# Spreading per-row values along the columns with VectorE's block transposes in place of matmuls with ones

## The chip, the cores and the metric

The kernel runs on one core of one Trainium2 chip. The time is device microseconds of one execution, start to end. Before the change three runs gave 2766.16, 2765.39 and 2765.9 us, median 2765.9. A profiled execution is looked at in detail; its own time was 2766.02 us, and the span from its first to its last instruction 2764.3 us.

## The reference, cut to what matters

128 graphs of 64 nodes with 512 features go through four layers; each layer is `x = layernorm(x + layer(x))`. Everything is float32. Three places take a value per node and need it once per row and once per column of the graph's 64x64 matrix:

```
# layer 0, a hypergraph convolution (twice): H = (adj != 0), D_i = sum_e H[i,e] * adj[0,e], B_e = sum_i H[i,e]
m   = 1/B[:, None] * (H^T @ (x @ W^T));   out = 1/D[:, None] * (H @ m) + b
# layer 1, scores of all pairs
y = x @ w;  s = y @ a
A = s[:, None] + s[None, :];  A = tanh(A / 8) * 8;  A = where(A >= 0, A, 0.1 * A)
A = exp(A) * adj
A = A / A.sum(-1, keepdims) * adj.sum(-1, keepdims)
out = A @ x @ w
# layer 2: three graph convolutions with relu; layer 3: attention with eight heads, adj and exp(-adj) added
```

The kernel keeps the graph matrices transposed (row: the node that is summed over; column: the node that receives), because a matmul sums over rows. So 1/D, the second s and the divisor of the row sums are all needed along the columns, while VectorE makes them as one value per partition.

## The kernel before

Two graphs lie on the 128 partitions (a pair), and four pairs make a group of 512 rows; 16 groups are worked in turn. A value per node is a tile `[128, 4]`, a graph matrix of a group `[128, 4, 64]`.

The products with the 512-wide weights are made in `multiply` (L551) in seven block products instead of eight: each block product is four matmuls of 128x128 by 256 columns, accumulated in PSUM tiles a, c and b (`a_l2c`, `c_l2c`, `b_l2c` for the product l2c, in the order B11, T1, T2, B21, T3, B22, T4). Between them VectorE or ScalarE takes snapshots (u) and sums out of PSUM, and a following block product on the same tile waits for that. PSUM has four such accumulators (pool `ps_acc`) and four more tiles (pool `ps_gt`) for transposes, graph products and the matrices of this change.

Three groups are in flight: side a (`first_half`) takes a group through layers 0 and 1, side b (`second_half`) takes the group before it through layer 2 and to the scores of layer 3, and t, the end of the same generator, finishes the group before that. A written list of steps (`order`, L1394) interleaves them; a step like a.ss is the stretch up to that `yield`. `start` does the same for the first group, where `strict` keeps TensorE, VectorE and ScalarE in the order of the text; in these parts the profile shows L132 for every instruction. After that a scheduler may move instructions on an engine against the text, by its own estimate of when operands are ready. `behind(key)` holds an instruction back: it is issued after the one recorded in `last_add` under that key.

How a value gets along the columns, in all three places: VectorE multiplies the identity (`identc`, L103, the unit matrix of each half stacked) with the value broadcast over 64 columns, which gives a diagonal matrix (`dg` L657 for 1/D, `e` L811 for the scores); TensorE multiplies it with `bones` (L93), a block matrix of ones, so every row gets the diagonal (`rbps` L663, `ss` L818); then it is taken out of PSUM (`rb` by ScalarE L668, or directly in the addition for `t`, L823). For the row sums of layer 1 the matmul with `bones` does the summing too: `den` (L831) sums t over its rows and gives each row the result, VectorE takes the reciprocal of all 128x256 (L836) and multiplies (L837). Group 0 does the scores and the division in two halves of two pairs (`attention`, `divided`).

```
t = tanh(ss + s4)          L823, L824
t = max(0.1 t, t)          L825
t = exp(8 t)               L826
t = t * atc                L827, atc: adj transposed
```

The steps around it in the steady list are

```
load a.w21 b.gh a.w2 rows b.l2c1 b.l2c2 a.ss b.l2c t.o1 a.den t.o2 a.c3 b.agg t.o a.p1 b.xT ... b.k1 prep b.k b.dots
```

`rows` makes the next group's H, its sums and 1/D (`prepare`, L618) and `prep` its `sps` and `smat`, the matrix of layer 0. a.c3 multiplies x by t (`gt_l`, L486); b.agg is layer 2's last sum over neighbours (L1148) and its addition to x (L1153); t.o is layer 3's output product (`a_wo`, `b_wo`, `c_wo`). The b side's addition out of c_l2c (L578) is `behind("e_...")`: VectorE does it after e of the other side. Weights come by SP's DMA queue into a ring of 20 tiles, asked for as tiles come free.

Of the kernel before, what the change touches and what calls it, by code (L numbers as in the profile page):

```python
# [41 lines left out]
def kernel(  # L42
# [48 lines left out]
    make_identity(nc, ident)  # L91

    bones = const.tile([P, 2, C], FP, name="bones")  # L93
    nc.vector.memset(bones, 0.0)
    nc.vector.memset(bones[0:C, 0, :], 1.0)
    nc.vector.memset(bones[C:P, 1, :], 1.0)
    ones = const.tile([P, P], FP, name="ones")
# [452 lines left out]

    def multiply(lefts, wt_q, dst, key, flipped=False, res=None, stops=(3,), then=None):  # L551

# [38 lines left out]
        last_add[f"{key}.p6"] = newest(PE)  # L591
        last_add[key] = vec.tensor_add(dst(0, 1), pc, s2).ins  # L592
        if then:
# [19 lines left out]
    def turned(t):  # L613

        return lambda m, n: t[:, 2 * n : 2 * n + 2, m * Q : (m + 1) * Q]


    def prepare(g):  # L618
# [24 lines left out]
        if q == 0:  # L643
            inverse(inv[:, 1], db[:, 1])
        else:
            by_rows()

            with behind(f"e_{q - 1}") if q > 2 else nullcontext():
                vec.tensor_mul(hn[:, 1], hn[:, 0], g["wb"])
                vec.reduce_sum(db[:, 0], hn[:, 1], axis=AX.X)  # L650
                inverse(inv, db)
        cs = small.tile([P, G], FP, name=f"cs_{q}", tag="cs")
        g["cs"], g["rowsum"] = cs, rowsum
        if q > 0:
# [6 lines left out]
        if q > 0:  # L661
            rb_ps = ps_gt.tile([P, G, C], FP, name=f"rbps_{q}", tag="gt")
# [70 lines left out]
    def first_half(g):  # L733
# [71 lines left out]
        for p in range(G):  # L805
# [4 lines left out]
        e = grp.tile([P, G, C], FP, name=f"e_{q}", tag="e", bufs=1)  # L810
        last_add[f"e_{q}"] = vec.tensor_mul(  # L811
            e, identc.unsqueeze(1).to_broadcast([P, G, C]), bcast(s4, G)
        ).ins
        yield "w2"

        ss = ps_gt.tile([P, G, C], FP, name=f"ss_{q}", tag="gt")
        with behind("l2c_0.p5") if q == 1 else nullcontext():
            ten.matmul(  # L818
                ss.rearrange("p a i -> p (a i)"), bones.rearrange("p g j -> p (g j)"),
                e.rearrange("p a i -> p (a i)"), start=True, stop=True,  # L820
            )
        t = grp.tile([P, G, C], FP, name=f"t_{q}", tag="t", bufs=1)
# [8 lines left out]
        ten.matmul(  # L831
            den.rearrange("p a i -> p (a i)"), bones.rearrange("p g j -> p (g j)"),
            t.rearrange("p a i -> p (a i)"), start=True, stop=True,
        )
        rd = grp.tile([P, G, C], FP, name=f"rd_{q}", tag="rd", bufs=1)
        vec.reciprocal(rd, den)  # L836
# [21 lines left out]
        with behind(f"q_{q - 1}.d"):  # L858
            rest()
        yield "ln1"  # L860


# [27 lines left out]
    def first_group(g):  # L890
# [71 lines left out]
        t = grp.tile([P, G, C], FP, name="t_0", tag="t", bufs=1)  # L962
        rd = grp.tile([P, G, C], FP, name="rd_0", tag="rd", bufs=1)
        mvs = [small.tile([P, 2, 2], FP, name=f"mv_l0_0_{d}", tag="mvp") for d in range(2)]
# [8 lines left out]
        def scored(d):  # L973
            rs = root(mvs[d], f"l0_0_{d}")
            vec.reciprocal(rs, rs)
            for p in range(2 * d, 2 * d + 2):
                normed(pair(p), mvs[d], rs, p % 2)
            for p in range(2 * d, 2 * d + 2):
                prod = work.tile([P, D], FP, name=f"xwa_0_{p}", tag="w")
                vec.scalar_tensor_tensor(  # L980
                    prod, pair(p), 1.0, wa_bc, ALU.mult, ALU.mult, accum_out=s4[:, p : p + 1]
                )
            at = slice(2 * d, 2 * d + 2)
            vec.tensor_mul(e[:, at], identc.unsqueeze(1).to_broadcast([P, 2, C]), bcast(s4[:, at], 2))

        def attention(d):
            at = slice(2 * d, 2 * d + 2)
            ss = ps_gt.tile([P, 2, C], FP, name=f"ss_0_{d}", tag="gt")
            ten.matmul(
                ss.rearrange("p a i -> p (a i)"), bones.rearrange("p g j -> p (g j)"),  # L990
                e[:, at].rearrange("p a i -> p (a i)"), start=True, stop=True,
            )
            vec.tensor_add(t[:, at], ss, bcast(s4[:, at], 2))
            act.activation(t[:, at], t[:, at], AF.Tanh, scale=0.125)
            vec.scalar_tensor_tensor(t[:, at], t[:, at], 0.1, t[:, at], ALU.mult, ALU.max)
            act.activation(t[:, at], t[:, at], AF.Exp, scale=8.0)
            vec.tensor_mul(t[:, at], t[:, at], g["atc"][:, at])

        def divided(d):
            at = slice(2 * d, 2 * d + 2)  # L1000
            den = ps_gt.tile([P, 2, C], FP, name=f"den_0_{d}", tag="gt")
            ten.matmul(
                den.rearrange("p a i -> p (a i)"), bones.rearrange("p g j -> p (g j)"),
                t[:, at].rearrange("p a i -> p (a i)"), start=True, stop=True,
            )
            vec.reciprocal(rd[:, at], den)
            vec.tensor_mul(t[:, at], t[:, at], rd[:, at])

# [12 lines left out]
        yield "w23"  # L1021
        divided(0)
        yield "den0"
        out_of_2(3, rows_of(3, hts, w2, 1, 2, ps))
# [8 lines left out]
        def out_of_l1(p):  # L1033
            ps = rows_of(p, [left.t], by_pairs[w_l1])
            vec.scalar_tensor_tensor(
                pair(p), ps.rearrange("p n f -> p (n f)"), g["rowsum"][:, p : p + 1], pair(p), ALU.mult, ALU.add
            )
            st = small.tile([P, 6], FP, name=f"st_l1_0_{p}", tag="st")
            stats(mvs[p // 2], st, p % 2, pair(p))
# [12 lines left out]
        yield "l11"  # L1052
        divided(1)
        yield "den1"
        normed_l1(0)
# [9 lines left out]
    def second_half(g):  # L1065
# [74 lines left out]
        for duo in range(2):  # L1140
# [3 lines left out]
            for h in range(2):  # L1144
                for p in range(2):
                    rows = slice(p * C, (p + 1) * C)
                    mat = g["atc"][rows, 2 * duo + p, :] if p == h else g["atx"][rows, duo, :]
                    ten.matmul(  # L1148
                        ps[p][h * C : (h + 1) * C, :], mat, g3[rows, 2 * duo + h, :], start=True, stop=True
                    )  # L1150
            for p in range(2):
                xr = xg[:, 2 * duo + p, :]
                vec.tensor_add(xr, ps[p], xr)  # L1153
        yield "agg"
# [226 lines left out]
    def taken(duo, ps, left):  # L1381
# [8 lines left out]
        a0.c1 prep0 keep0 rest a0.w1a keep1 a0.w1b rows0 bw0 a0.c20 wa bw0 a0.c21 doubled0 constant0 rows1 a0.w20 keep2 wa  # L1390
        a0.w21 prep1 a0.w22 a0.ss0 a1.c1 a0.w23 a0.den0 doubled1 a0.w24 a0.c30 a1.w1a1 a0.l10 a0.ss1 a0.l11 a0.den1 a1.w1a2
# [62 lines left out]
    for n, (who, q, name) in enumerate(todo):  # L1454
# [7 lines left out]
        elif who == "rows":  # L1462
            if q > 0:
                preps[q] = prepare(groups[q])
            with behind(f"l0w2_{q - 1}" if q > 2 else "q_0") if q > 1 else nullcontext():
                next(preps[q])
        elif who == "prep":
            next(preps[q])
# [93 lines left out]
```

## Time and profile before

| | |
|---|---|
| median of three runs | 2765.9 us |
| the profiled execution, and its span | 2766.02, 2764.3 us |
| TensorE busy, share of the span | 2743.0 us, 99% |
| VectorE | 2024.8 us, 73% |
| ScalarE | 808.2 us, 29% |
| one step of the steady list (the product l0w of one group to that of the next, 996.83 to 1167.37 and 1167.37 to 1337.13 in the chain) | about 170 us |
| granted TensorE clock | 1.0 |

An f32 matmul leaves two records on TensorE. A record's duration includes what the pipeline overlaps with the next, so the time that a matmul costs is read from start to start. "PE" is TensorE, "DVE" VectorE, "ACT" ScalarE, "PEld" the loading of weights into TensorE. A name like `t<-ss,s` is output and inputs; buffer and group numbers are left out.

### The profile page before, as it was taken

How to read it: one execution, taken by the hardware profiler on the slowest of the kernel's cores; microseconds unless marked ns; L12 is line 12 of the kernel's file. 1: busy time of each engine (PE TensorE's matmuls, PEld its weight loads, DVE VectorE, ACT ScalarE, POOL GpSimd, SP SyncE). 2: the span in 40 equal slices, each digit the busy share in tenths (PEclk: the TensorE clock that was granted, in tenths of full speed). 3: DMA queues.
4: the chain of work that ended last, by engine and by line, in shares of the span. 5: the costliest groups of instructions: out<-in, count | busy, mean ns of one | idle time of the engine just before them, and what ended most of it. 6: DMA issues, size and time to landing. Idle time of an engine off the chain costs nothing.

```text
span 2764.3 us, 67699 instructions
## 1 busy us (share of the span) xinstructions
PE 2743.0 (99%) x28868; PEld 2364.3 (86%) x28868; DVE 2024.8 (73%) x3883; ACT 808.2 (29%) x1459; POOL 38.0 (1%) x71
## 2 busy tenths in 40 slices
PE   9999999999999999999999999999999999999998
PEld 7888888888888888888888888888888888888887
DVE  6868687776777777777776767778777687776766
ACT  3223223232232322322233232232322323132232
POOL 2000000000000000000000000000000000000000
PEclk9999999999999999999999999999999999999999
DMA  8535454454544545445454454545545454454541
GB/s 270 171 119 157 128 170 135 138 165 133 166 127 141 165 127 168 128 145 165 132 164 130 142 161 132 162 126 152 158 135 164 131 156 145 127 165 130 150 124 61
DMA packets 309388, 405.15 MB, mean 147 GB/s; under 512 B 57408, under 2 KB 185184, under 8 KB 309088
## 3 DMA queue, kind: packets, MB, share of 16 engines
q1 hardware_dynamic: 304256, 385.58, 47.4%
q0 software_dynamic: 4832, 15.24, 1.5%
q8 instruction: 229, 3.75, 0.6%
q14 instruction: 71, 0.58, 0.1%
HBM read 369.78 MB, written 30.93 MB: 145 GB/s over the span
## 4 chain that ended last, share of the span: by engine, by line
PE 98%; DVE 1%; ACT 0%; issue 0%; DMA 0%; DVEq 0%
PE a_l0w L544 15%; PE b_l0w L544 7%; PE a_l2b L544 4%; PE a_q L544 4%; PE a_k L544 4%; PE a_l2c L544 4%; PE a_l2a L544 4%; PE a_v L544 4%; PE c_l0w L544 4%; PE a_l1w L544 4%; PE a_wo L544 4%; PE gt_l L486 3%; PE pp L132 3%; PE gt_l0h L486 2%; PE b_l2b L544 2%; PE b_q L544 2%
## 5 line engine op out<-in xcount | busy, mean ns | idle before, releaser
L544 PE MATMUL a_l0w<-w2w,aT_l0h 128*128 128x256 f32 x720 | 164.3, 381 | 0.0
L462 DVE BATCH_NORM_STATS2 st_l<-x 128x6 f32<-128x512 f32 x244 | 157.4, 671 | 0.1
L544 PEld LDWEIGHTS a_l0w<-w2w,aT_l0h 128*128 128x128 f32 x720 | 135.6, 190 | 18.8
L468 DVE TENSOR_SCALAR x<-x,mv_l,rs_l 128x512 f32<-128x512 f32 x244 | 119.1, 541 | 1.8
L544 PE MATMUL b_l0w<-w2w,s_l0h 128*128 128x256 f32 x480 | 108.5, 379 | 0.0
L763 ACT ACTIVATE h<-h 128x1024 f32<-128x1024 f32 (+1 forms) x58 | 54.9, 947 | 178.5 <-DVE h L592 157.5
L497 ACT COPY aT_l<-gt_l 128x512 f32<-128x512 f32 x148 | 78.4, 596 | 81.5 <-PE gt_l L486 81.5
L544 PEld LDWEIGHTS b_l0w<-w2w,s_l0h 128*128 128x128 f32 x480 | 91.1, 190 | 12.5
L1122 ACT ACTIVATE aT_h<-gth,gb_col 128x256 f32<-128x256 f32 x128 | 48.5, 492 | 159.0 <-PE gth L1114 159.0
L452 ACT ACTIVATE rs_l<-mv_l,eps_t 128x4 f32<-128x4 f32 (+1 forms) x64 | 19.1, 298 | 253.6 <-DVE mv_l L463 241.8
L559 DVE TENSOR_TENSOR u_l0w<-a_l0w,b_bc 128x512 f32<-128x512 f32 x56 | 38.5, 688 | 69.3 <-PE a_l0w L544 69.3
L544 PE MATMUL a_l2b<-gwbw,aT_h 128*128 128x256 f32 x360 | 86.6, 383 | 0.7 <-ACT aT_oT L1384 0.7
L544 PE MATMUL a_l2c<-gwcw,aT_h 128*128 128x256 f32 x360 | 86.6, 383 | 0.4 <-DVE g L584 0.4
L544 PE MATMUL a_q<-aT_xT,wqw 128*128 128x256 f32 x360 | 85.1, 379 | 0.7 <-ACT aT_xT L1172 0.7
L544 PE MATMUL a_l1w<-ww,aT_l 128*128 128x256 f32 x360 | 85.1, 379 | 0.2 <-ACT aT_l L497 0.2
L544 PE MATMUL a_l2a<-aT_l,gwaw 128*128 128x256 f32 x360 | 85.0, 379 | 0.0
L544 PE MATMUL a_k<-aT_xT,wkw 128*128 128x256 f32 x360 | 85.0, 379 | 0.0
L544 PE MATMUL a_l0w<-w1aw,aT_l 128*128 128x256 f32 x336 | 80.8, 383 | 0.0
L544 PE MATMUL a_v<-wvw,aT_xT 128*128 128x256 f32 x336 | 80.8, 383 | 0.0
L544 PE MATMUL a_wo<-wow,aT_oT 128*128 128x256 f32 x336 | 79.5, 379 | 0.1
L544 PE MATMUL a_l0w<-w1bw,aT_l 128*128 128x256 f32 x336 | 79.4, 379 | 0.0
L544 PEld LDWEIGHTS a_l2c<-gwcw,aT_h 128*128 128x128 f32 x360 | 66.4, 190 | 13.3 <-DVE g L584 3.7
(537 smaller groups left out, 6487.8 us busy)
## 6 DMA issues: line engine op xcount, KB each, us to landing
w2w<-w2k SPq DMA_DIRECT2D x210, 256.0 KB, 2.7
x<-in_x_dram SPq DMA_DIRECT2D x15, 1024.0 KB, 6.7
w1aw<-w1ak SPq DMA_DIRECT2D x60, 256.0 KB, 2.7
w1bw<-w1bk SPq DMA_DIRECT2D x60, 256.0 KB, 2.7
ww<-wk SPq DMA_DIRECT2D x60, 256.0 KB, 2.8
gwaw<-gwak SPq DMA_DIRECT2D x60, 256.0 KB, 3.9
gwbw<-gwbk SPq DMA_DIRECT2D x60, 256.0 KB, 2.6
gwcw<-gwck SPq DMA_DIRECT2D x60, 256.0 KB, 2.7
```

The costliest lines, as they stand in the source:

```text
L132: return op(*args, **kwargs)
L452: act.activation(rs[:, at], mv[:, at, 1], AF.Sqrt, bias=eps_t)
L462: vec.bn_stats(st, xg[:, p, :])
L468: vec.tensor_scalar(xg[:, p, :], xg[:, p, :], mv[:, p, 0:1], rs[:, p : p + 1], ALU.subtract, ALU.mult)
L486: ten.matmul(ps[g][f * C : (f + 1) * C, c, p, :], src(2 * duo + p)[rows, c0 : c0 + C], mat[rows, 2 * duo + p, :], start=True, stop=True,)
L497: act.copy(o[:, :, :, g, :], ps[g])
L544: ten.matmul(acc[:, blk, :], lhsT, rhs, start=(first and blk == 0 and i == 0), stop=(last and i == n_k - 1), skip_group_check=True,)
L559: last_add[f"{key}.{what}"] = (act.copy(t, ps) if res is None else vec.tensor_add(t, ps, res(m, n))).ins
L763: act.activation(hn, hn, AF.Relu)
L1122: act.activation(o[:, :, h, :], ps[h][:, c].rearrange("p (d a) i -> p d (a i)", d=2), AF.Relu, bias=gb2_col[:, k : k + 1],)
```

## The change

A new function `along(dst, src)` lays a value per node along the columns with VectorE alone. VectorE's transpose turns blocks of 32x32. `along` transposes the value, broadcast over 64 columns, for all 128 partitions at once: each block of 32 rows then has its own 32 values in both halves of its columns. Half of these blocks are right. Four more transposes, each of 32 partitions, overwrite the others with the values of the other 32 rows of the same graph.

It takes the place of the three matmuls: of `dg` and `rbps` and the copy for 1/D, of `e` and `ss` for the scores, and, for the divisor, VectorE multiplies exp's result also by `adn` (adj as it is; the scores are symmetric), sums along the columns (four values per partition), takes the reciprocal of those and lays them out. `bones` is gone. Group 0 doesn't lay the divisor out at all: `row_ratio` makes row sum over divisor per node, and the row scale that is applied after the product takes it.

The order changes with it. The 1/D part of `rows` becomes a step of its own, `rows2`, behind b.agg (for groups from 3 on); the points that hold work back move: the key `e_q` now marks the addition of t, and the addition that takes b_l2c out is held behind t's division. a.den comes before b.l2c, and group 1's a.c3 goes behind group 0's agg matmuls.

```diff
+    def along(dst, src):
+        n, B = src.shape[1], 32
+        vec.transpose(dst, bcast(src, n))
+        for g in range(2):
+            for b in range(2):
+                here, there = (slice(g * C + k * B, g * C + (k + 1) * B) for k in (b, 1 - b))
+                done = vec.transpose(
+                    dst[there, :, b * B : (b + 1) * B], src[here].unsqueeze(2).to_broadcast([B, n, B])
+                )
+        return done
...
# multiply
-        last_add[key] = vec.tensor_add(dst(0, 1), pc, s2).ins
+        with behind(held):
+            last_add[key] = vec.tensor_add(dst(0, 1), pc, s2).ins
...
# prepare
-            with behind(f"e_{q - 1}") if q > 2 else nullcontext():
+            if q > 2:
+                yield
+            with behind(f"agg_{q - 2}") if q > 2 else nullcontext():
...
-            dg = grp.tile([P, G, C], FP, name=f"dg_{q}", tag="dg", bufs=1)
-            vec.tensor_mul(dg, identc.unsqueeze(1).to_broadcast([P, G, C]), bcast(inv[:, 0], G))
+            rb = grp.tile([P, G, C], FP, name=f"rb_{q}", tag="rb", bufs=1)
+            along(rb, inv[:, 0])
...
-            ten.matmul(
-                rb_ps.rearrange("p a t -> p (a t)"), bones.rearrange("p g j -> p (g j)"),
-                dg.rearrange("p a t -> p (a t)"), start=True, stop=True,
-            )
-            rb = grp.tile([P, G, C], FP, name=f"rb_{q}", tag="rb", bufs=1)
-            act.copy(rb, rb_ps)
...
# first_half
-        last_add[f"e_{q}"] = vec.tensor_mul(
-            e, identc.unsqueeze(1).to_broadcast([P, G, C]), bcast(s4, G)
-        ).ins
+        along(e, s4)
+        t = grp.tile([P, G, C], FP, name=f"t_{q}", tag="t", bufs=1)
+        last_add[f"e_{q}"] = vec.tensor_add(t, e, bcast(s4, G)).ins
...
-            ten.matmul(
-                ss.rearrange("p a i -> p (a i)"), bones.rearrange("p g j -> p (g j)"),
-                e.rearrange("p a i -> p (a i)"), start=True, stop=True,
-            )
-        vec.tensor_add(t, ss, bcast(s4, G))
...
+        tn = grp.tile([P, G, C], FP, name=f"tn_{q}", tag="tn", bufs=1)
+        vec.tensor_mul(tn, t, g["adn"])
         vec.tensor_mul(t, t, g["atc"])
         yield "ss"
-        den = ps_gt.tile([P, G, C], FP, name=f"den_{q}", tag="gt")
-        ten.matmul(
-            den.rearrange("p a i -> p (a i)"), bones.rearrange("p g j -> p (g j)"),
-            t.rearrange("p a i -> p (a i)"), start=True, stop=True,
-        )
+        den = small.tile([P, G], FP, name=f"den_{q}", tag="den")
+        vec.reduce_sum(den, tn, axis=AX.X)
+        vec.reciprocal(den, den)
         rd = grp.tile([P, G, C], FP, name=f"rd_{q}", tag="rd", bufs=1)
-        vec.reciprocal(rd, den)
-        vec.tensor_mul(t, t, rd)
+        along(rd, den)
+        last_add[f"t_{q}"] = vec.tensor_mul(t, t, rd).ins
...
-            graph_T(pair, t, left.t, duo, f"l1_{q}", both=q > 1)
+            with behind("agg_0.p") if q == 1 else nullcontext():
+                graph_T(pair, t, left.t, duo, f"l1_{q}", both=q > 1)
...
# second_half
-        gen = multiply([h2], (w_g[2], q), nat(g3), f"l2c_{q}", stops=(3, 5))
+        gen = multiply([h2], (w_g[2], q), nat(g3), f"l2c_{q}", stops=(3, 5), held=f"t_{q + 1}")
...
# the list
-        t.osum a.c2a b.l2b a.c2b b.gb3 load a.w21 b.gh a.w2 rows b.l2c1 b.l2c2 a.ss b.l2c t.o1 a.den t.o2 a.c3 b.agg t.o
+        t.osum a.c2a b.l2b a.c2b b.gb3 load a.w21 b.gh a.w2 rows b.l2c1 b.l2c2 a.ss a.den b.l2c t.o1 t.o2 a.c3 b.agg rows2 t.o
```

More of the change, by code (lines that the diff above doesn't have):

```diff
@@ L91 @@
     make_identity(nc, ident)
[L93 to L96, printed above, removed]
     ones = const.tile([P, P], FP, name="ones")
@@ L549, in product, with multiply @@
         stream.done(*wt_q, what)
-    def multiply(lefts, wt_q, dst, key, flipped=False, res=None, stops=(3,), then=None):
+    def multiply(lefts, wt_q, dst, key, flipped=False, res=None, stops=(3,), then=None, held=None):
         acc = [ps_acc.tile([P, 2, Q], FP, name=f"{n}_{key}", tag="acc") for n in "ab"]
@@ L660, in prepare @@
         yield
-        if q > 0:
-            rb_ps = ps_gt.tile([P, G, C], FP, name=f"rbps_{q}", tag="gt")
-            ten.matmul(
-                rb_ps.rearrange("p a t -> p (a t)"), bones.rearrange("p g j -> p (g j)"),
-                dg.rearrange("p a t -> p (a t)"), start=True, stop=True,
-            )
-            rb = grp.tile([P, G, C], FP, name=f"rb_{q}", tag="rb", bufs=1)
-            act.copy(rb, rb_ps)
         sm = grp.tile([P, G, C], FP, name=f"smat_{q}", tag="smat", bufs=2)
@@ L810, in first_half @@
         e = grp.tile([P, G, C], FP, name=f"e_{q}", tag="e", bufs=1)
-        last_add[f"e_{q}"] = vec.tensor_mul(
-            e, identc.unsqueeze(1).to_broadcast([P, G, C]), bcast(s4, G)
-        ).ins
+        along(e, s4)
+        t = grp.tile([P, G, C], FP, name=f"t_{q}", tag="t", bufs=1)
+        last_add[f"e_{q}"] = vec.tensor_add(t, e, bcast(s4, G)).ins
         yield "w2"
-        ss = ps_gt.tile([P, G, C], FP, name=f"ss_{q}", tag="gt")
-        with behind("l2c_0.p5") if q == 1 else nullcontext():
-            ten.matmul(
-                ss.rearrange("p a i -> p (a i)"), bones.rearrange("p g j -> p (g j)"),
-                e.rearrange("p a i -> p (a i)"), start=True, stop=True,
-            )
-        t = grp.tile([P, G, C], FP, name=f"t_{q}", tag="t", bufs=1)
-        vec.tensor_add(t, ss, bcast(s4, G))
         act.activation(t, t, AF.Tanh, scale=0.125)
@@ L860, in first_half, with row_ratio @@
         yield "ln1"
+    def row_ratio(g, tn, at):
+        n = tn.shape[1]
+        ratio = small.tile([P, n], FP, name=f"ratio_{g['q']}_{at.start}", tag="ratio")
+        vec.reduce_sum(ratio, tn, axis=AX.X)
+        vec.reciprocal(ratio, ratio)
+        vec.tensor_mul(ratio, ratio, g["rowsum"][:, at])
+        return ratio
     def doubled(g):
@@ L962, in first_group @@
         t = grp.tile([P, G, C], FP, name="t_0", tag="t", bufs=1)
-        rd = grp.tile([P, G, C], FP, name="rd_0", tag="rd", bufs=1)
+        tn = grp.tile([P, G, C], FP, name="tn_0", tag="tn", bufs=1)
+        ratios = {}
         mvs = [small.tile([P, 2, 2], FP, name=f"mv_l0_0_{d}", tag="mvp") for d in range(2)]
@@ L983, in scored @@
             at = slice(2 * d, 2 * d + 2)
-            vec.tensor_mul(e[:, at], identc.unsqueeze(1).to_broadcast([P, 2, C]), bcast(s4[:, at], 2))
+            along(e[:, at], s4[:, at])
         def attention(d):
             at = slice(2 * d, 2 * d + 2)
[L988 to L993, printed above, removed]
+            vec.tensor_add(t[:, at], e[:, at], bcast(s4[:, at], 2))
             act.activation(t[:, at], t[:, at], AF.Tanh, scale=0.125)
@@ L996, in attention @@
             act.activation(t[:, at], t[:, at], AF.Exp, scale=8.0)
+            vec.tensor_mul(tn[:, at], t[:, at], g["adn"][:, at])
             vec.tensor_mul(t[:, at], t[:, at], g["atc"][:, at])
[L999 to L1007, printed above, removed]
+            ratios[d] = row_ratio(g, tn[:, at], at)
         w2 = by_pairs[w_2]
@@ L1021, in first_group @@
         yield "w23"
-        divided(0)
-        yield "den0"
         out_of_2(3, rows_of(3, hts, w2, 1, 2, ps))
@@ L1035, in out_of_l1 @@
             vec.scalar_tensor_tensor(
-                pair(p), ps.rearrange("p n f -> p (n f)"), g["rowsum"][:, p : p + 1], pair(p), ALU.mult, ALU.add
+                pair(p), ps.rearrange("p n f -> p (n f)"), ratios[p // 2][:, p % 2 : p % 2 + 1], pair(p), ALU.mult, ALU.add
             )
@@ L1052, in first_group @@
         yield "l11"
-        divided(1)
-        yield "den1"
         normed_l1(0)
@@ L1150, in second_half @@
                     )
+            last_add[f"agg_{q}.p"] = newest(PE)
             for p in range(2):
                 xr = xg[:, 2 * duo + p, :]
-                vec.tensor_add(xr, ps[p], xr)
+                last_add[f"agg_{q}"] = vec.tensor_add(xr, ps[p], xr).ins
         yield "agg"
@@ L1390 @@
         a0.c1 prep0 keep0 rest a0.w1a keep1 a0.w1b rows0 bw0 a0.c20 wa bw0 a0.c21 doubled0 constant0 rows1 a0.w20 keep2 wa
-        a0.w21 prep1 a0.w22 a0.ss0 a1.c1 a0.w23 a0.den0 doubled1 a0.w24 a0.c30 a1.w1a1 a0.l10 a0.ss1 a0.l11 a0.den1 a1.w1a2
+        a0.w21 prep1 a0.w22 a0.ss0 a1.c1 a0.w23 doubled1 a0.w24 a0.c30 a1.w1a1 a0.l10 a0.ss1 a0.l11 a1.w1a2
         a0.c31 a1.w1a keep3 a1.resid a0.l12 a1.w1b1 a0.l13 a1.w1b2 b0.gt a1.w1b
@@ L1466 @@
                 next(preps[q])
-        elif who == "prep":
+        elif who in ("prep", "rows2"):
             next(preps[q])
```

## The prediction

> **What bounds the kernel now.** I read the page's busy times and its chain first, then the answers for the tiles that the change touches, then the order of time through one steady group (group 5's layer 1 beside group 4's layer 2).
>
> ```profile
> span 2764.3 us, 67699 instructions
> ...
> PE 2743.0 (99%) x28868; PEld 2364.3 (86%) x28868; DVE 2024.8 (73%) x3883; ACT 808.2 (29%) x1459; POOL 38.0 (1%) x71
> ...
> PE 98%; DVE 1%; ACT 0%; issue 0%; DMA 0%; DVEq 0%
> ```
>
> TensorE is busy 99% of the span and holds 98% of the chain that ended last. Every matmul taken off it is worth its issue time, unless a new wait takes its place. VectorE is 73% busy: room in the mean, not in every stretch.
>
> ```profile
> L818 PE MATMUL ss<-e,bones x30: 379/379/483, 191.1 to 2563.5; 128*128 128x256 f32 x30
> ...
>   DVE e L811: 3.2, 13
> ```
>
> The tile of the scores' sums: 15 matmuls, two records each, and 13 short waits for VectorE's e (3.2/13 = 0.24 us). The matmul of the row sums (den) and that of 1/D (rbps) read the same: 30 records each at a median of 379 ns. For the reciprocal, the tile rd:
>
> ```profile
> L836 DVE RECIPROCAL rd<-den x15: 1756/1757/1758, 196.0 to 2569.6; 128x256 f32<-128x256 f32 x15
> ```
>
> In order of time (start, us, engine, line):
>
> ```profile
> 860.06 1.89 PE L544 MATMUL a_l2c<-gwcw,s_h 128*128 128x256 f32 x8
> ...
> 861.32 0.43 DVE L811 TENSOR_TENSOR e<-identc,s 128x256 f32<-128x256 f32 x1
> ...
> 861.79 0.70 PE L818 MATMUL ss<-e,bones 128*128 128x256 f32 x2
> ...
> 861.99 0.69 DVE L578 TENSOR_TENSOR g<-c_l2c,u_l2c 128x512 f32<-128x512 f32 x1
> ...
> 862.33 0.59 PE L544 MATMUL b_l2c<-gwcw,s_h 128*128 128x256 f32 x2
> ...
> 867.62 0.59 PE L831 MATMUL den<-t,bones 128*128 128x256 f32 x2
> ...
> 868.05 1.89 PE L544 MATMUL b_wo<-wow,s_oT 128*128 128x256 f32 x8
> ...
> 869.78 1.89 PE L544 MATMUL a_wo<-wow,s_oT 128*128 128x256 f32 x8
> ...
> 871.60 2.10 PE L486 MATMUL gt_l<-t,x 64*64 64x64 f32 x128
> ...
> 879.31 0.69 DVE L584 TENSOR_TENSOR x<-a_wo,u_wo 128x512 f32<-128x512 f32 x1 [1.04 <-PE a_wo L544]
> ...
> 880.83 1.89 PE L544 MATMUL a_wo<-wow,aT_oT 128*128 128x256 f32 x8
> ```
>
> Durations overlap, so starts are what count: four matmuls (eight records) take 869.78 - 868.05 = 1.73 us, 0.432 each. ss holds TensorE for 862.33 - 861.79 = 0.54 (0.43 and 0.10 of waiting), den for 0.43. The a_l2c product before den took 1.83 instead of 1.73, waiting for VectorE's g. On VectorE, a 128x256 product lasts 0.42 and lets the next begin after 0.34; one of 512 columns 0.69 and 0.60.
>
> [...] No transpose is in this trace; a 128x128 product of f32 lasts 291 ns in it (group 0's e). [...]
>
> **The change, part by part.**
>
> Removed from TensorE: 15 matmuls each of ss, den and rbps, and four half-wide ones of group 0. 45 x 0.432 = 19.4 us; in group 0 den starts at 78.65 and the next matmul at 78.87, so 4 x 0.22 = 0.9. Two waits go too: 0.10 at ss and 0.10 before den, in 14 groups, 2.8. Gross gain 23.1.
>
> Removed from VectorE, by free-to-free time: e 0.34, dg 0.34, the wide reciprocal about 1.68. From ScalarE, rb's copy (0.38), off the path. Four PSUM tiles fewer in ps_gt relax its ring; no wait there is visible, so nothing for that.
>
> Added to VectorE: three column layouts per group (function along), each one transpose over 128 partitions x 256 and four of 32 x 128. The first: 0.42 + 0.02 = 0.44, and 0.04 until a dependent operation begins (as e after the accumulator's read). The four: 0.31 less the 0.08 that neighbours overlap, 0.23 each, the last to its end 0.31. Together 0.48 + 3 x 0.23 + 0.31 + 0.04 = 1.52 until a dependent operation begins, 1.4 of VectorE's time. Bounds: [...] above, half the rate for 4-byte elements, about 2.2. I take 1.52. Also tn (0.34), its reduction (0.35) and a short reciprocal (0.15). Net on VectorE: 4.2 + 0.84 - 2.36, some 2.7 us a group of 170, where it idles some 45: no bound in the mean. What matters is what queues behind.
>
> Moved: the row work of 1/D (hn, db, inv, rb, hb) from beside the scores to behind layer 2's last sums (behind agg), about 3.3 us of VectorE with its layout. Its operands were loaded a step before, so it waits for no transfer. It does release two: wb and adn are read by it, or are queued with what it reads, and SP issues the next group's wb after hn's product. SP's order moves with it, from among wq's loads to behind wk's fourth, where the following weight tile waits for a later matmul (a_wo) anyway; the ring of 20 tiles stands a product chain ahead, so nothing for that. POOL's queue is as it was. cs goes later still, with a step of slack.
>
> Now the new order on TensorE in a steady group: a_l2c (T2), the four b_l2c, two of b_wo, a_l2c (T3), two b_wo, one a_wo, a_l2c (T4), three a_wo, gt_l.
>
> First new wait: b_wo needs an accumulator, and all four are taken until VectorE has read c_l2c (g L578). That read stands behind e's record, which is now t's addition. From e at 861.32: 1.52, the addition 0.34, then g from 863.18 to 863.87, and 0.06 to TensorE (g L584 ended 865.73, a_l2c began 865.79): 863.93. TensorE arrives at 860.06 + 2 x 1.73 = 863.51. It waits 0.42. At the lower layout cost it waits 0.3, at the upper 1.1.
>
> t for gt_l: VectorE from 863.8: u_wo 0.60, t's maximum 0.34, after exp (0.42) tn, t, reduction, reciprocal, to about 866.6; g (a_l2c) 0.6, the first transpose, u_wo 0.6, the four, the product: t at about 869.7. TensorE gets to gt_l at 863.93 + 4 x 1.73 + 0.1 = 870.9 (0.1 as from 869.78 + 1.73 to 871.60). A cover of 1.2 us hides the whole chain; without it each us late costs one. The addition that takes b_l2c out (L592) now stands behind that product (held) and ends at about 870.1; agg, its first reader, starts at 872.7, and c_wo, which may need its accumulator, at 874.9.
>
> gt_l thus moves from 871.60 to 870.9, 0.7 earlier. After it VectorE's four agg additions end at about 876.4. Then hn 0.34, db with its wait 0.47, x from c_wo 0.60, the three steps of inv 0.63, the transpose 0.37, hb 0.34, four transposes 0.92, 3.67 in all: x from a_wo (L584), begun at 879.31 before, begins at 880.1 and ends 880.8. TensorE's last a_wo reads over that accumulator. TensorE starts c_wo at 875.55 - 0.7 = 874.85, a_wo 1.83 later (as before: 877.38), then b_wo 1.73, one a_l1w put ahead 0.43: it is there at 874.85 + 1.83 + 2 x 1.73 + 0.43 = 880.57, and may go on at 880.85. Second new wait: 0.3, in the 13 steps that prepare a next group (3 to 15); upper end 1.0, lower 0.1. What is late next, s_l for b_l1w, still has over 1.5 us, and xtp's normalized rows over 0.7.
>
> Sum: gross 23.1, less 14 x 0.42 = 5.9, less 13 x 0.3 = 3.9: 13.3. Group 1 has another order; there t's chain waits for exp behind wqt's sums, and I count no gain beyond its matmuls. At the start, VectorE's layouts delay smat (70.04) by about 1.8 us, which ends as gt_l needs it (73.07): 0.1 or nothing. The profiled execution took 2766.0, 0.1 from the median of 2765.9; 2766.0 - 13.3 = 2752.7, say 2753.
>
> **Rivals.** (a) The two waits don't form: the whole 23.1 comes, 2743. For it: both waits are below half a microsecond and rest on sums of short intervals. Against: c_l2c's read stands behind five transposes by order, and TensorE arrives within a product of it. (b) The layouts are slow: if 4-byte transposes go at half rate, each layout takes 0.7 more, and it comes through at both waits: (14 + 13) x 0.7 = 18.9, 2772. It decides from 13.3/27 = 0.5 us more per layout, that is from about 2.0. For it: the trace has no transpose, [...] (c) Half of that, 0.35 more per layout: 9.5 given back, 2762, within the noise. (d) VectorE becomes the bound: 2.7 us against 45 idle, no.
>
> **How the numbers follow.** Forecast 0.62, with its own range 2748 to 2759; (a) 0.15, (b) 0.13, (c) 0.10. About 0.2%, 5.5 us, is what a measurement can tell from no change. Faster: the forecast and (a), with a little of them lost to the border, 0.77; same 0.10; slower 0.13. Range: the lower end takes (a) in, 2743; the upper leaves out (b), 2766.
>
> **What would show it.** TensorE's busy time about 20 us lower; no ss, den, rbps. A transpose of 128x256 at about 0.44 us and of 32x128 at about 0.31. A wait of b_wo on g L574 (the new number of L578) and one of the last a_wo on x L580, 0.3 to 0.4 us each; gt_l of layer 1 without a wait for t. Wrong, if the small transposes last over 0.45 us, if gt_l waits for t (the cover of 1.2 is gone), or if waits show at xtp or b_l1w.

## The result, and the profile after

The changed kernel took 2763.28 us (median of 12 runs, 2762.07 to 2764.66), the kernel before 2765.35 beside it (12 runs, 2762.78 to 2767.41): ratio 0.9993, 95% interval 0.9984 to 1.0002. No difference can be told. 2753 was forecast; 2763.28 is inside the range on record (2743 to 2766) but outside the forecast's own (2748 to 2759). The profiled execution took 2763.43 us, with a span of 2761.7.

The page of the changed kernel: span, busy times, shares of the chain that ended last.

```profile
span 2761.7 us, 67726 instructions
...
PE 2726.4 (99%) x28770; PEld 2346.2 (85%) x28770; DVE 2074.4 (75%) x4117; ACT 801.8 (29%) x1444; POOL 37.6 (1%) x71
...
PE 85%; DVE 13%; issue 1%; ACT 1%; DMA 0%; DVEq 0%
```

TensorE does 98 records fewer and is busy 16.6 us less, but the span shrank by only 2.6. The rest has turned into waiting. The chain says on whom: it was 98% on TensorE and now runs over VectorE for 13% of the span. That is not 13% of loss; the chain steps over to VectorE at each short wait and follows its queue back for some microseconds before it returns.

The tile of the scores' layout (line, operation, count, shortest/median/longest in ns), changed kernel:

```profile
L622 DVE STREAM_TRANSPOSE e<-s x60: 299/302/308, 190.0 to 2561.8; 32x128 f32<-32x128 f32 x60
L618 DVE STREAM_TRANSPOSE e<-s x15: 445/445/446, 189.6 to 2560.4; 128x256 f32<-128x256 f32 x15
```

Both durations, 0.302 and 0.445 us, are near what the prediction took (0.31 and 0.44), which no run had shown then. What TensorE waits for, in the changed kernel (total us, times, longest):

```profile
PE b_wo L539 <- DVE g L574: 6.8, 13, 1.1
PE a_wo L539 <- DVE x L580: 6.6, 13, 0.5
...
PE a_l2c L539 <- ACT u_l2c L555: 1.8, 1, 1.8
```

Both forecast waits are there, 13 times each, with the forecast releasers; a third, in group 1, is new too. In order of time (start, us, engine, line), the same group as in the prediction:

```profile
860.55 1.89 PE L539 MATMUL a_l2c<-gwcw,s_h 128*128 128x256 f32 x8
...
861.80 0.45 DVE L618 STREAM_TRANSPOSE e<-s 128x256 f32<-128x256 f32 x1
862.28 1.89 PE L539 MATMUL b_l2c<-gwcw,s_h 128*128 128x256 f32 x8
862.28 1.25 DVE L622 STREAM_TRANSPOSE e<-s 32x128 f32<-32x128 f32 x4
863.57 0.42 DVE L817 TENSOR_TENSOR t<-e,s 128x256 f32<-128x256 f32 x1
863.91 0.68 DVE L574 TENSOR_TENSOR g<-c_l2c,u_l2c 128x512 f32<-128x512 f32 x1
...
864.65 1.13 PE L539 MATMUL b_wo<-wow,s_oT 128*128 128x256 f32 x4 [0.48 <-DVE g L574]
...
865.61 1.89 PE L539 MATMUL a_l2c<-gwcw,aT_h 128*128 128x256 f32 x8
...
877.28 0.41 DVE L660 TENSOR_TENSOR hn<-hn,wb 128x256 f32<-128x256 f32 x1
...
880.06 1.25 DVE L622 STREAM_TRANSPOSE rb<-inv 32x128 f32<-32x128 f32 x4
...
881.34 0.69 DVE L580 TENSOR_TENSOR x<-a_wo,u_wo 128x512 f32<-128x512 f32 x1
...
882.09 1.99 PE L539 MATMUL a_wo<-wow,aT_oT 128*128 128x256 f32 x8 [0.51 <-DVE x L580]
```

Four small transposes of 0.302 us take 1.25 us together: they start 0.314 apart (1.25 less the last one's length, over three) and overlap nothing. The layout runs from 861.80 to 863.57, 1.77 us. b_l2c has 862.28 to 864.65, 2.37 us, where four matmuls take 1.73: the first wait costs 0.64 from start to start. Then b_wo's two matmuls hold 864.65 to 865.61, 0.96 instead of 0.86: the product that TensorE had to wait for runs 0.10 longer. From hn to x out of a_wo VectorE works 4.06 us.

Where the time went is read by adding up, for each product tile, the intervals from the start of each of its records on TensorE to the next start, whatever tile that belongs to:

| TensorE, us from start to start | changed less before |
|---|---|
| ss, rbps, den | -8.37, -7.88, -7.16 |
| a_k, after which rbps used to come | +1.31 |
| a_l2c, b_wo, a_wo (a product longer by 0.10 after a wait) | -1.20, +1.45, +1.60 |
| the product before b_wo (b_l2c; before the change in part b_wo itself) | +10.29 |
| a_l1w, the product before a_wo | +8.73 |
| gt_l, agg, pp, b_l0w, sps | -2.54, -1.16, +0.93, +0.71, +0.70 |
| all | -2.58 |

b_l2c's 10.29 are 13 times 0.63 to 0.71, in the 13 groups that wait for g, and 1.91 in group 1 (read below). The last row but one has irregular intervals among short matmuls; gt_l sums to 101.9 before and to 99.4 after, and to between 97.4 and 101.0 in the runs below. No cause is claimed for them.

### The profile page after: what moved, and what is told of

Its sections match the earlier page's. It is cut to its first block, busy times and chain, and to the rows that moved or that the text cites. A ratio compares the mean times of both kernels' runs of the same rounds, so it can differ in the third digit from the quotient of the medians.

```text
span 2761.7 us, 67726 instructions
## 1 busy us (share of the span) xinstructions
PE 2726.4 (99%) x28770; PEld 2346.2 (85%) x28770; DVE 2074.4 (75%) x4117; ACT 801.8 (29%) x1444; POOL 37.6 (1%) x71
## 4 chain that ended last, share of the span: by engine, by line
PE 85%; DVE 13%; issue 1%; ACT 1%; DMA 0%; DVEq 0%
PE a_l0w L539 13%; PE b_l0w L539 7%; PE a_l2b L539 4%; PE a_l2a L539 4%; PE a_v L539 4%; PE c_l0w L539 4%; PE a_k L539 4%; PE a_q L539 4%; PE a_l1w L539 3%; PE gt_l L481 3%; PE a_l2c L539 2%; PE gt_l0h L481 2%; PE a_wo L539 2%; PE b_l2b L539 2%; PE b_l1w L539 2%; PE b_l2a L539 2%
## 5 line engine op out<-in xcount | busy, mean ns | idle before, releaser
L539 PEld LDWEIGHTS a_wo<-wow,aT_oT 128*128 128x128 f32 x336 | 62.8, 190 | 19.4 <-DVE x L580 10.9
```

The source lines that it names most:

```text
L539: ten.matmul(acc[:, blk, :], lhsT, rhs, start=(first and blk == 0 and i == 0), stop=(last and i == n_k - 1), skip_group_check=True,)
```

## Experiments

Ratios are to the kernel before, run beside each, with 95% intervals. The kernel before has medians from 2764.28 to 2765.35 in the sets of runs, and the changed kernel stands in the first set alone, so a difference between an experiment and its 2763.28 is uncertain by about 1 us. Theory A: each wait is the length of what is queued ahead of one reading on VectorE, and nothing else holds TensorE there. Rival B: another limit stands close behind, so a wait taken away comes back elsewhere.

**The 1/D work later.** In `prepare` and the list of steps:

```diff
-            with behind(f"agg_{q - 2}") if q > 2 else nullcontext():
+            with behind(f"l1w_{q - 1}.d") if q > 2 else nullcontext():
...
-        ... b.agg rows2 t.o a.p1 b.xT ...
+        ... b.agg t.o a.p1 rows2 b.xT ...
```

> The 1/D work of the next group goes behind layer 1's last addition instead of agg's, so that nothing stands between the agg additions and x from a_wo on VectorE. Theory A (each of the two new waits is set by what is queued ahead of one reading, and TensorE has nothing else to wait for): the waits a_wo <- x (6.6 us in 13) vanish and b_wo <- g stays at about 6.8; the starts of a_l1w to a_wo gave back 8.7 us and about 1.4 more went into restarts, so the time falls from 2763.3 by 8 to 10, to 2753 to 2755. Rival B (TensorE has a second limit a little behind the first, so that a wait taken away turns up at the next one): 2761 to 2764, with new waits of about 0.5 us at c_wo, xtp or l1w.

2761.05 us (21 runs), ratio 0.9987 (0.9981 to 0.9994). A's time is missed by 6. The waits of a_wo did go: a_l1w -8.72 and a_wo -1.35 from start to start. But 13 new ones appear, of a_q for qT. The row of the list of waits, then one of them in order of time:

```profile
PE a_q L539 <- DVE qT L580: 4.1, 13, 0.3
...
906.54 0.69 DVE L580 TENSOR_TENSOR qT<-a_q,u_q 128x512 f32<-128x512 f32 x1
...
907.28 1.99 PE L539 MATMUL a_q<-aT_xT,wqw 128*128 128x256 f32 x8 [0.32 <-DVE qT L580]
```

b_q, the product before, gains 6.23 and a_q 1.36: 7.6 of the 10.1 come back. VectorE works nearly without a gap from rb's four small transposes at 894.83 to qT 12 us later, so 1/D's work delays that reading as it had delayed x. It is B in effect, with its time, though not on a tile that it named: moving this piece of work moved its wait.

**g ahead of e's transposes.** The key `e_q`, behind which g reads c_l2c, goes to the last score sum:

```diff
-            vec.scalar_tensor_tensor(
+            last_add[f"e_{q}"] = vec.scalar_tensor_tensor(
                 prod, xg[:, p, :], 1.0, wa_bc, ALU.mult, ALU.mult, accum_out=s4[:, p : p + 1]
-            )
+            ).ins
...
-        last_add[f"e_{q}"] = vec.tensor_add(t, e, bcast(s4, G)).ins
+        vec.tensor_add(t, e, bcast(s4, G))
```

> The reading of c_l2c (g) is held behind the last score sum and no longer behind t's addition, so VectorE does it before the five transposes of e. Theory A: b_wo no longer waits for g (6.8 us in 13 before this edit, 9.0 from start to start, and some 1.4 of restarts), group 1's wait of 1.8 for u_l2c goes too; T4 may wait up to 0.1 for the a_l2c reading; a_wo <- x stays at 6.6. Time 2751 to 2755. Rival B (t is then late for gt_l, whose cover of 0.9 us is used up, or the wait turns up at another product): gt_l waits for t by 0.5 to 0.7 us in 14 groups and the time stays at 2761 to 2764.

2759.72 us (16 runs), ratio 0.9981 (0.9973 to 0.9988). b_wo's waits go, all but one of 1.4 in group 2, but the scheduler gives TensorE another order (order of time):

```profile
865.02 1.97 PE L539 MATMUL a_l2c<-gwcw,aT_h 128*128 128x256 f32 x8
...
866.82 1.03 PE L539 MATMUL b_l2c<-gwcw,s_h 128*128 128x256 f32 x4
867.09 0.69 DVE L580 TENSOR_TENSOR g<-a_l2c,u_l2c 128x512 f32<-128x512 f32 x1 [0.16 <-PE a_l2c L539]
...
867.84 1.99 PE L539 MATMUL a_l2c<-gwcw,aT_h 128*128 128x256 f32 x8
869.67 1.89 PE L539 MATMUL b_wo<-wow,s_oT 128*128 128x256 f32 x8
```

T3 (865.02) and T4 (867.84) write the same accumulator, with only half of b_l2c between them: 1.02 us for two matmuls that take 0.86. T4 waits for the reading between (g, which ends at 867.78), and T3 and T4 take 1.80 and 1.83 instead of 1.73: 0.33 a group, of which the waits list shows nothing. Groups 1 and 2 wait 1.83 and 0.48 for t, and group 1 also 0.98 for g. gt_l of the other groups does not wait for t, so B's first reason is wrong, its second right: the wait turned up at another product. The time lies between the two forecasts, 1.3 us below B's.

**Both edits.**

> Both edits: the 1/D work behind layer 1's last addition and g ahead of e's transposes. Theory A (the two waits are separate and add up): about 23 us of matmuls leave and next to nothing comes back, 2742 to 2746, TensorE's waits for VectorE as few as before the change. Rival B (a further limit of TensorE or VectorE stands behind): less than the sum of the two single gains, 2752 or more, with a new wait that takes the place of the two.

2758.29 us (11 runs), ratio 0.9974 (0.9965 to 0.9983). The two gains nearly add up (2.2 and 3.6 against the changed kernel, 5.0 together), and the new waits stay: a_q 4.1 in 13 again, T3 and T4 as in the last run. A's 2742 to 2746 is missed; B's time and its new waits are there. That the gains add up to 0.8 less than the sum of the two can't be told from noise.

**The split of `rows` undone,** the 1/D work back beside the scores, behind t's addition:

```diff
-            if q > 2:
-                yield
-            with behind(f"agg_{q - 2}") if q > 2 else nullcontext():
+            with behind(f"e_{q - 1}") if q > 2 else nullcontext():
...
-        ... a.c3 b.agg rows2 t.o
+        ... a.c3 b.agg t.o
```

> The change with one part undone: the 1/D work stays beside the scores, held behind t's addition as before behind e, with its layout by transposes. Theory A (place in VectorE's queue decides): the wait a_wo <- x goes (gain of 9 to 10), but about 3.5 us of VectorE work now stands between the scores and the readings that b_wo, T4 and gt_l wait for, where gt_l had 0.9 us of cover: 1.5 to 3 us more per group in 13 groups, so 2775 to 2800. Rival B (VectorE has room there, and the split was not needed): 2752 to 2756.

2774.34 us (5 runs), ratio 1.0034 (1.0022 to 1.0046), just below A's 2775 to 2800, and far from B. The work now delays the readings that b_wo and T4 need (waits):

```profile
PE a_l2c L539 <- DVE g L580: 10.8, 12, 0.9
PE b_wo L539 <- DVE g L574: 9.8, 12, 0.8
```

gt_l hardly waits for t, where A had looked for part of the loss. Without the split the change would have cost 9 us against the kernel before (2765.04 beside it); the split was needed.

**A cheaper layout, nothing moved.** The value goes into two columns per pair by five small copies, then one transpose lays both halves along:

```diff
-        vec.transpose(dst, bcast(src, n))
+        made.append(n)
+        two = small.tile([P, n, 2], FP, name=f"two_{len(made)}", tag=f"two{n}")
+        vec.tensor_copy(two, src.unsqueeze(2).to_broadcast([P, n, 2]))
...
-                done = vec.transpose(
-                    dst[there, :, b * B : (b + 1) * B], src[here].unsqueeze(2).to_broadcast([B, n, B])
-                )
-        return done
+                vec.tensor_copy(two[there, :, b], src[here])
+        return vec.transpose(
+            dst.rearrange("p a (b t) -> p (a b) t", b=2),
+            two.rearrange("p a b -> p (a b)").unsqueeze(2).to_broadcast([P, 2 * n, B]),
+        )
...
+    made = []
```

> The order of the change stays and only the layout gets cheaper: the value is put into two columns per pair by one 128-partition copy and four copies of 32 partitions x 4, and one transpose of 128x256 lays both halves along, instead of four more transposes of 32x128. At some 0.1 us per small copy the layout takes 1.0 us instead of 1.77. Theory A (the waits are the layout's length, 0.64 and 0.67 us a group from start to start, and nothing else stands behind them in this order): both waits shrink by some 0.75 and vanish, with their restarts: 17.7 + 3 us, and up to 1 in group 1, so 2741 to 2746. Rival B (a further limit takes the place of each wait, as in the two runs that moved work): 2756 to 2761, with new waits on other tiles. Between, if the small copies cost 0.2 each: along 1.5, waits of 0.3, 2751 to 2755.

2755.75 us (7 runs), ratio 0.9970 (0.9959 to 0.9981): not A's 2741 to 2746, because a copy of 32x4 takes 0.160 us, not the 0.1 that the expectation assumed, and again the next begins only 0.17 after it. (The kernel before already showed that a small VectorE instruction is not that short: a reciprocal of 128x4 takes 0.18 in it.) Order of time, first the first wait and what follows it, then the second:

```profile
859.11 0.17 DVE L620 COPY two<-s 128x8 f32<-128x8 f32 x1
859.31 0.69 DVE L624 COPY two<-s 32x4 f32<-32x4 f32 x4
859.58 1.89 PE L539 MATMUL b_l2c<-gwcw,s_h 128*128 128x256 f32 x8
860.03 0.45 DVE L625 STREAM_TRANSPOSE e<-two 128x256 f32<-128x256 f32 x1
860.51 0.42 DVE L822 TENSOR_TENSOR t<-e,s 128x256 f32<-128x256 f32 x1
...
861.59 0.70 PE L539 MATMUL b_wo<-wow,s_oT 128*128 128x256 f32 x2
...
863.85 1.03 PE L539 MATMUL b_wo<-wow,s_oT 128*128 128x256 f32 x4
864.08 0.68 DVE L580 TENSOR_TENSOR g<-a_l2c,u_l2c 128x512 f32<-128x512 f32 x1
...
864.81 2.00 PE L539 MATMUL a_l2c<-gwcw,aT_h 128*128 128x256 f32 x8
...
866.64 0.59 PE L539 MATMUL b_wo<-wow,s_oT 128*128 128x256 f32 x2
...
876.40 1.89 PE L539 MATMUL b_wo<-wow,s_oT 128*128 128x256 f32 x8
...
877.66 0.69 DVE L580 TENSOR_TENSOR x<-a_wo,u_wo 128x512 f32<-128x512 f32 x1
878.27 0.44 DVE L625 STREAM_TRANSPOSE rb<-two 128x256 f32<-128x256 f32 x1
878.41 2.00 PE L539 MATMUL a_wo<-wow,aT_oT 128*128 128x256 f32 x8
```

The layout is 1.40 us, 0.37 shorter. The first wait is 861.59 - 859.58 - 1.73 = 0.28 (0.64 before this edit): 0.36 less for a layout 0.37 shorter, in all 13 groups alike, and group 1's wait falls by 0.36 too (b_l2c -5.15, 14 times 0.36 in the main). The second, from b_wo's start to a_wo's, is 2.01 - 1.73 = 0.28 (0.67 before, a_l1w -8.73). Its 0.39 is not the layout's alone: the transpose of 0.44 now comes after x, and TensorE no longer puts a matmul of a_l1w (0.43) between; the two nearly cancel.

The waits shrink as the layout does, which is A's mechanism, at the size that its middle case gave for slow copies (2751 to 2755), 0.75 above it. A small part comes back elsewhere, as B had it: T4 (864.81) now follows two matmuls of b_wo and waits for the reading of T3 (g, which ends at 864.76), so these two take 0.96 instead of 0.86, and T4 1.83 instead of 1.73. a_l2c takes 1.36 us more in all, and b_wo some 1.7 (its 5.38 less the 13 waits of 0.28 that now fall after it). That is why the medians fall by 7.5 and not by 14 times 0.36 and 13 times 0.39 (10.1).

**1/D's work in VectorE's gaps,** with g ahead of e as above: sums and reciprocals stay behind agg, the transposes go behind x from a_wo (a further step, rows3, after t.o):

```diff
+            if q > 2:
+                yield
             rb = grp.tile([P, G, C], FP, name=f"rb_{q}", tag="rb", bufs=1)
-            along(rb, inv[:, 0])
+            with behind(f"wo_{q - 3}.d") if q > 2 else nullcontext():
+                along(rb, inv[:, 0])
```

> As the run with both edits, but the 1/D work isn't moved as one piece: its sums and reciprocals stay behind agg, where VectorE idles 1.4 us waiting for c_wo and a_wo, and its five transposes go behind x from a_wo, where it idles another 1.03 us ahead of b_wo. Theory A (a piece of VectorE work costs what it exceeds the idle time at its place): the 13 waits of a_q for qT (0.48 from start to start and 0.10 of restart each, 7.6 us) go and nothing takes their place, 2758.3 - 7.6: 2749 to 2753. Rival B (they turn up again, at b_l1w or xtp): 2757 to 2760.

2749.70 us (5 runs), ratio 0.9948 (0.9935 to 0.9960): A. The 13 waits of a_q are gone (b_q -6.22, a_q -1.36 against the run with both edits), and none came for them. The same work, cut so that each piece fits where VectorE waited for TensorE anyway, costs no wait that the list shows.

**T4 after a_wo.** The step that ends l2c moves behind two steps of layer 3's output product:

```diff
# second_half
-        with behind("exp_1") if q == 0 else nullcontext():
-            whole(gen)
+        with behind("exp_1") if q == 0 else nullcontext():
+            next(gen)
+        yield "l2c3"
+        with behind(f"wo_{q - 1}.p2"):
+            whole(gen)
         yield "l2c"
...
# the list
-        ... a.den b.l2c t.o1 t.o2 a.c3 ...
+        ... a.den b.l2c3 t.o1 t.o2 b.l2c a.c3 ...
```

> The previous one, and the last block product of l2c (T4) comes after b_wo and a_wo instead of two halves of B22 after T3, which it must wait for VectorE to read. Theory A: another 0.15 of waiting and 0.10 of restart in 14 groups, 3.5 us, so 2746 to 2750. Rival B: gt_l or agg then wait for the reading of T4 or for t, and it is 2750 to 2756.

2751.81 us (5 runs), ratio 0.9955 (0.9943 to 0.9968), a miss for A: B, at gt_l (waits; groups 1 and 2, which waited for t in the previous run too, are among the 15).

```profile
PE gt_l L481 <- DVE t L836: 7.4, 15, 1.8
```

a_wo is done earlier, so VectorE's queue has its reading u_wo (869.26) ahead of t's product (869.87), and t is 0.6 later than it could be; gt_l begins at 870.34 after a wait of 0.34.

**That with the cheaper layout.**

> The previous one with the cheaper layout. Theory A: there are no waits for VectorE left to take away in the steady groups, so no more than 0 to 2 us against the previous run (group 1's and the start's share): 2744 to 2748. Rival B (waits too short to be listed remain): 2740 to 2743.

2744.34 us (5 runs), ratio 0.9929 (0.9916 to 0.9941): the fastest, 19.9 us below the kernel before and 18.9 below the changed one. The number is A's, but not by A's reasoning: it is 7.5 below the previous run instead of 0 to 2, since the previous run still had t's wait. With e's and rd's layouts both 0.37 shorter, t's product comes ahead of the reading u_wo from a_wo, and 13 waits go (a_l2c, the product before gt_l, -4.07). The rest of the 7.5 is spread over b_l2c (-1.89), a_wo (-0.93) and others; no cause is claimed for it. The chain is 95% on TensorE and 4% on VectorE. Only groups 1 and 2 wait for t, 2.8 us together.

**Each layout cut short by itself,** the written order kept: the four small transposes left out, once of the scores' layout, once of 1/D's. `along` gets a third argument, and one call passes it:

```diff
+        for g in range(0 if whole else 2):
...
-        along(e, s4)
+        along(e, s4, True)
```

> The change with the four small transposes of the scores' layout left out (groups 1 to 15; the score matrix then lacks its off-diagonal 32x32 blocks), order kept: e's layout falls from 1.77 to 0.48 us, everything else is as in the change. Theory A (the wait of b_wo for g is this layout's length and nothing is behind it in this order): b_wo's 13 waits go, 9.0 us and 1.5 of restarts, and 1.3 of group 1's 1.8; a_wo <- x stays at 6.6: 2763.3 - 10.5 to 11.8, so 2750 to 2754. Rival B (taking this wait away uncovers another in every case, as it did where g was moved): 2758 to 2761.

2753.69 us (5 runs), ratio 0.9958 (0.9946 to 0.9971), A. From its waits:

```profile
PE a_wo L539 <- DVE x L580: 6.7, 13, 0.5
...
PE a_l2c L539 <- ACT u_l2c L555: 0.5, 1, 0.5
```

b_wo waits no more (its row is gone, b_l2c -10.31), the other wait stays as it was, and group 1's falls from 1.8 to 0.5, by the 1.3 of the four transposes. The scheduler also puts T3 ahead of b_wo here. That isn't what takes the wait away: in the same group g ends at 862.10, and b_l2c is done at 862.80, where b_wo stood before.

> The change with the four small transposes of 1/D's layout left out (groups 1 to 15; rb then lacks its off-diagonal blocks), order kept. Theory A: a_wo's 13 waits for x go, 8.7 us and 1.4 to 1.6 of restarts; b_wo <- g stays at 6.8 in 13: 2752 to 2755. Rival B (another wait follows, as where the 1/D work was moved): 2759 to 2762.

2751.43 us (5 runs), ratio 0.9949 (0.9935 to 0.9963), 0.6 below A's 2752 to 2755. Here the other wait stays, b_wo for g, 6.9 us in 13. a_l1w loses 8.73 and a_wo 1.35, the expected amounts; the rest is in gt_l, sps and pp (2.0, 0.75 and 0.65), the irregular ones among them. B falls for both: each wait goes with the layout that stands ahead of its reading, and the other stays. If the two gains add up (9.6 + 11.8 = 21.4 us, no run has both), they and the changed kernel's own 2.1 make 23.5, next to the 23.1 counted for the matmuls.

## Why the prediction was wrong, step by step

The places, the releasers and the direction were right, the sizes were not: a forecast gain of 13.3 us came out as 2.1 in the medians and 2.6 in the spans.

**Gross gain, 23.1: right.** ss, rbps and den give 23.4 back, less the 1.31 that a_k takes over, plus the 1.20 at a_l2c: 23.3.

**The layout, 1.52: the step that failed.** "The four: 0.31 less the 0.08 that neighbours overlap, 0.23 each" took the overlap from products over 128 partitions. The durations held, to 0.01 us, the overlap didn't exist: 0.314 apart, three times 0.084 = 0.25 more, 1.77. The bounds (1.4 to 2.2) held it, but the middle was put near the end where everything overlaps.

No row of the trace before shows an instruction of 32 partitions, but one shows two of 64. `smat` is made by two products, one on the first 64 partitions and one on the others (kernel before, in order of time):

```profile
912.82 1.92 DVE L468 TENSOR_SCALAR x<-x,mv_l,rs_l 128x512 f32<-128x512 f32 x4
914.65 0.87 DVE L680 TENSOR_TENSOR smat<-sps,rb 64x256 f32<-64x256 f32 x2
```

The first begins 0.09 before its neighbour on all 128 partitions ends (914.74), so having fewer partitions does not by itself prevent an overlap. The two last 0.41 and 0.43 and take 0.87 together: the second starts 0.03 after the first has ended, though what it reads from TensorE was ready at 914.46. Nor is it the transpose that prevents an overlap. In the changed kernel one over all 128 partitions ends at 879.74, and its neighbour begins 0.08 earlier:

```profile
879.29 0.45 DVE L618 STREAM_TRANSPOSE rb<-inv 128x256 f32<-128x256 f32 x1
879.66 0.38 DVE L670 TENSOR_TENSOR hb<-ht,inv 128x256 f32<-128x256 f32 x1
```

What the small transposes, the small copies and the second `smat` have in common is that each works on other partitions than the one before it. The row that could have warned of the missing overlap was there before the change.

No run had shown the durations that the prediction took for one transpose; the runs since then do: 311 ns for 128x128 (group 0 of the run with the cheaper layout), 445 for 128x256, 302 for 32x128. So 128 columns more cost a transpose 445 - 311 = 134 ns, as much as a product: 425 - 291 = 134 (e, before the change).

**First wait, 0.42: 0.64.** From e's start TensorE arrived after 2.21 us (2.19 forecast), g began after 2.11 (1.86), b_wo 0.74 after that (0.75). The whole difference is the layout's 0.25. The wait came in 13 groups and not in 14: 8.3 us in all instead of 5.9, 2.4 more. The cheaper layout shows that it is the layout's length: 0.37 less of it took 0.36 off the wait in each of the 13.

**Second wait, 0.3: 0.67.** b_wo's product begins at 879.26 and the last a_wo at 882.09, 2.83 later, with five matmuls between the two starts (four of b_wo, one of a_l1w: 1.73 + 0.43 = 2.16). VectorE took 4.06 us for the work ahead of x instead of 3.67, and 0.36 of that difference are the four small transposes, 1.28 instead of 0.92. 13 times 0.37, 4.8 us.

**A term left out: 0.10 more for the product after each wait.** The prediction had this 0.10 on the side of the gains (at a_l2c, for g) and didn't put it on the side of the new waits. b_wo and a_wo took 1.45 and 1.60 more, 3.05 us.

**Group 1, "no gain beyond its matmuls": a loss of 1.9.** Kernel before, then changed kernel, each in order of time:

```profile
188.67 0.59 ACT L559 COPY u_l2c<-a_l2c 128x512 f32<-128x512 f32 x1 [2.87 <-PE a_l2c L544]
...
189.31 1.99 PE L544 MATMUL a_l2c<-gwct,aT_h 128*128 128x256 f32 x8
...
192.46 0.42 ACT L824 ACTIVATE t<-t 128x256 f32<-128x256 f32 x1 [1.91 <-DVE t L823]
```

```profile
191.79 0.42 ACT L819 ACTIVATE t<-t 128x256 f32<-128x256 f32 x1 [4.03 <-DVE t L817]
192.12 0.57 ACT L555 COPY u_l2c<-a_l2c 128x512 f32<-128x512 f32 x1
...
192.74 1.99 PE L539 MATMUL a_l2c<-gwct,aT_h 128*128 128x256 f32 x8 [1.77 <-ACT u_l2c L555]
```

After the change tanh (L819) sits ahead of the copy of a_l2c in ScalarE's queue and waits for t, and t for the transposes; T3 waits for the copy. In the kernel before, that copy ran ahead of tanh. From start to start it is 1.91 (in b_l2c's row above), and 1.29 less of transposes took 1.28 off it in the run with the score layout cut short. The prediction followed what had moved through the queues of VectorE, SP and POOL, not through ScalarE's.

Together 2.4 + 4.8 + 3.05 + 1.9 = 12.15 lost against the forecast, and the irregular rows of the table give 1.36 back (their sum): 13.3 - 12.15 + 1.36 = 2.5 of the 2.6 in the spans. The overlap that wasn't there is 7.2 of the 12.15; the two terms that the sum had at nothing are the other 5. That the irregular rows gave 1.36 back is luck.

**t for gt_l, cover 1.2: right in sign.** t is ready at 870.88, gt_l starts at 871.75: 0.87 left, no wait.

**The rivals.** (c), layouts 0.35 longer, 2762, came nearest, with 0.25 and 0.36 measured, but was given 0.10; (b), half rate, is refuted by the 445 ns; (a), no waits at all, is nearly what the fastest run reached by cheaper layouts and another order (2744.34).

What isn't settled: whether the partitions read or those written decide if two VectorE instructions overlap, for both change in the second `smat` and in the small transposes and copies after the first; why a product takes 0.10 longer after a wait; and why the irregular intervals of gt_l differ between kernels by more than the change itself moved.

## What to carry to other kernels

In this kernel two engines run in lockstep. There the price of work added to the slower queue is not its mean but what it adds ahead of each reading that the full engine needs next: find that reading, count the cover in tenths of a microsecond, and put an instruction's latency without any overlap at one end of the range. Look in the trace for instructions that change partitions as the new ones will, and not only for ones of the same size. Moving such work moved the wait with it; cutting it into pieces that fit the gaps where its engine waits anyway, and making it shorter, is what paid (2749.70 and 2744.34 here, against 2763.28).

## What the runs showed of the hardware

VectorE instructions that follow each other on other partitions did not overlap here. Transposes of 32x128 lasted 0.302 us and started 0.314 apart, copies of 32x4 lasted 0.160 and started 0.17 to 0.18 apart, and the second of two 64-partition products (`smat`) started 0.03 after the first had ended, where products over 128x256 last 0.42 and start 0.34 apart. A 32-partition transpose of 128 columns lasted nearly as long as one over all 128 partitions (302 against 311 ns).

A product of TensorE that begins after a wait for another engine took some 0.10 us longer (1.83 instead of 1.73 for four matmuls), at b_wo, a_wo, a_q and a_l2c alike; a new wait should be priced with it. It is not a mark of a wait, though: in the kernel before, the products that follow the 64x64 matmuls of gt_l0h take 0.10 longer as well and wait for nothing that the list shows: the 15 of four matmuls 1.83 or 1.84 (c_l2b from 647.76 to the next product at 649.59), the 15 of eight 3.55 or 3.56, where others take 3.45 (a_l0w from 656.89 to 660.45, b_l0w from there to 663.90).
